# An attention layer's step table: one comparison per unit on VectorE in place of a subtraction on GpSimd and a clamp

## The chip, the cores and the metric

The kernel runs on one core of one Trainium2 chip. The metric is the device time of one launch, in microseconds; the number quoted is the median of three runs. In the profile, PE is TensorE's matmuls and PEld its weight loads, DVE is VectorE, ACT is ScalarE, POOL is GpSimd and SP is the engine that issues most transfers. L423 means line 423 of the kernel's source.

## What is computed

Four graph layers run one after the other over 16 batches of 1024 nodes with 128 features and a sparse adjacency matrix (about 0.8% of the entries, and the diagonal). After each layer comes a residual and a layer norm. The change touches the first layer, an attention over edges:

```python
h_self = x @ W_self + b_self
h_nb = x @ W_nb + b_nb
pre = (h_self @ A1_i)[:, :, None, :] + (h_nb @ A1_j)[:, None, :, :] + A1_b
scores = (relu(pre) @ A2_w)[..., 0] + A2_b[0]
scores = where(adj == 0, -1e9, scores)
attn = softmax(scores, axis=-1)
out = relu(h_self + einsum("bij,bjf->bif", attn, h_nb))
x = layernorm(x + out)
```

## The kernel before

The attention works on edges and not on the full matrix. The 1024 nodes of a batch are cut into 10 groups of 104 rows. A *unit* is a pair of groups (i, j) with j at or after i; 11 units make a *block* (two rows of the triangle of pairs), 5 blocks make a batch, and so there are 80 blocks. For each unit the edges between the two groups are packed into at most 128 slots. For that the kernel counts the edges in each row, turns the counts into running offsets (`off`, one number per row and unit, written by `copy_offsets` from PSUM), and builds from them a *step table* `g`: for each row and each of 128 slots, 1 where the slot lies beyond the row's offset and 0 otherwise. A matmul with a difference matrix (`steps`, L464) turns the step table into a one-hot table: which row owns which slot. A second matmul and a comparison (`others`, `copy_others`, L488) give the other end of each edge; `widen` (L494) makes both tables wider for the gather.

With these tables a unit is worked through as follows: `gather` (L554, L559) fetches the projected features of both ends of 128 edges with matmuls into a PSUM tile `pg`, of which there are three; `score` (L571, DVE) makes the scores; `weigh` (L581, L583, ACT) takes the exponential and multiplies; `scatter` (L592, PE) adds the weighted rows into three PSUM banks, using a table `we` that `numbered` makes (L539, DVE).

Beside this, the next batch is prepared: `mask_rows` (L316, L318, POOL) turns loaded adjacency rows into a 0/1 mask that is kept and stored, `projection` (L343 to L371) makes the features. And the batch before is ended: `collect` (L603), `end_divide`, `end_group` (L636, L639, and the row statistics of L78 and L79), `end_root` (POOL), `end_norm` (ACT), transposes and stores. The ending falls into the first three blocks of the following batch.

The order on every engine is written out by hand. Each piece of work is put into a list with `do(slot, key, f, ...)`; one slot is one unit, and the key is the place in slots from the block's start. The list is sorted by this place (L803), the instructions are emitted in that order, and `as_traced` ties each engine to it. For the block two ahead (`x + 2`) the constants of the change stand here: `BEYOND` (L157) places the subtraction `beyond` (L419, instruction L423 on POOL) and `CLAMP` (L158) the clamp `clamp` (L428, instruction L431 on DVE). Both work in three pieces of 4, 4 and 3 units, that is 512, 512 and 384 columns on 105 partitions. Of `g` there is one buffer, so the first subtraction of a block waits until the last `steps` matmul of the block before has read it. `off` is float32, `k_next` (the numbers 1 to 128 in every partition) and `g` are float16.

```python
BEYOND = (3.72, 5.65, 6.42)
CLAMP = (6.38, 8.56, 11.15)
```

Of the kernel before, what the change touches and what calls it, by code (L numbers as in the profile page):

```python
# [17 lines left out]
ALU = mybir.AluOpType  # L18
# [74 lines left out]
NG, W, C = 10, 104, 128  # L93
NP = NG * W
E = W + 1
# [10 lines left out]
def band(r):  # L106

    return [(i, j) for i in (r, NG - 1 - r) for j in range(i, NG)]
# [45 lines left out]
PROJECT = (  # L154
    (6.25, 6.42, 6.54, 7.25, 7.33, 6.85, 16.48), (9.85, 9.9, 10.6, 9.95, 11.38, 11.56, 17.53),
)
BEYOND = (3.72, 5.65, 6.42)  # L157
CLAMP = (6.38, 8.56, 11.15)  # L158
NUMBERED = (1.38, 5.32, 9.9)
ONE_WAY = (-2.25, 5.95)  # L160
WIDEN = (3.38, 6.02, 8.53)
# [16 lines left out]
def phase_att(ctx, tc, t, c, x1_d, x1T_d, mask_d, keep, flags):  # L178

    nc = tc.nc  # L180
# [10 lines left out]
    def load(name, shape, dtype=F16):  # L191
        w = (cp if name == "k_id" else ep).tile(shape, dtype, name=name)
        nc.sync.dma_start(w, t[name])
        return w
# [12 lines left out]
    k_next = load("k_next", [P, C])  # L207
# [178 lines left out]
    def pieces():  # L386
        return [(n0, min(4, UNITS - n0)) for n0 in range(0, UNITS, 4)]

    def block(x):

        if x not in V and x < B * BANDS:
            v = V[x] = Consts()
            v.x = x
            b, v.r = divmod(x, BANDS)
            v.d, v.mt, v.q, v.todo = S[b], MT[b % 2], QS[x % 2], band(v.r)
        return V.get(x)
# [22 lines left out]
    def beyond(v, n0, m):  # L419

        if n0 == 0:
            v.g = sm.tile([P, UNITS, C], F16, name="g", bufs=1)
        nc.gpsimd.tensor_tensor(  # L423
            v.g[:E, n0 : n0 + m, :], k_next[:E].unsqueeze(1).to_broadcast([E, m, C]),
            v.off[:, n0 : n0 + m].unsqueeze(2).to_broadcast([E, m, C]), ALU.subtract,
        )

    def clamp(v, n0, m):  # L428

        g = v.g[:E, n0 : n0 + m, :]  # L430
        nc.vector.tensor_scalar(g, g, 1.0, 0.0, op0=ALU.min, op1=ALU.max)  # L431

    def ranks(v, n0, m, pw):

# [16 lines left out]
    def one_way(v, half):  # L451

        i = (v.r, NG - 1 - v.r)[half]
        at, nb = half * (NG - v.r), NG - i
        junk = sm.tile([P, NG, W], BF16, name="one_way", bufs=1)
        nc.vector.scalar_tensor_tensor(  # L456
            junk[:W, :nb, :], v.q[:W, at : at + nb, :W], EDGE,
            v.mt[:W, i, i * W : NP].rearrange("p (n w) -> p n w", w=W),
            op0=ALU.is_ge, op1=ALU.not_equal, accum_out=seen_one_way[:W, v.x, half : half + 1],
        )  # L460
# [32 lines left out]
    def widen(v, n0, m):  # L493
        nc.scalar.copy(v.ends[:W, n0 : n0 + m], v.o[:W, n0 : n0 + m])  # L494
# [21 lines left out]
    def bank_products(parts):  # L516

        bank = ps_w.tile([P, 512], F32, name="pw")
        at = 0
        for kind, k, v in parts:  # L520
            f, g = PARTS[kind]
            args = pieces()[k] if kind in ("step", "other", "rank") else ()
            f(v, *args, bank[:, at:])
            held[kind, k, v.x] = lambda g=g, v=v, args=args, to=bank[:, at:]: g(v, *args, to)
            at += TAKES.get(kind, 384)
# [176 lines left out]
    def do(slot, key, f, *args):  # L702
        todo.append((slot + key, len(todo), f, args))
# [39 lines left out]
    for x in range(-3, B * BANDS):  # L743
        b, r = divmod(x, BANDS)
        at = x * UNITS
        for u in range(UNITS if x >= 0 else 0):
            do(at + u, 0.2, open_gather, b, r, u)
            do(at + u, SCORE, take, score, b, r, u)
            do(at + u, WEIGH, take, weigh, b, r, u)
            do(at + u, SCATTER, scatters, b, r * UNITS + u)  # L750
        for k in range(3 if x >= 0 else 0):
            do(at, NUMBERED[k], numbered, b, r, *CHUNKS[k])
        for key, parts in BANKS:
            parts = [(kind, k, x + AHEAD[kind]) for kind, k in parts if 0 <= x + AHEAD[kind] < B * BANDS]
            if parts:
                do(at, key, lambda parts: bank_products([(kind, k, block(y)) for kind, k, y in parts]), parts)
                for kind, k, y in parts:
                    do(at, READ[kind, k], lambda *key: held.pop(key)(), kind, k, y)
        for k in range(3):
            if 0 <= x + 2 < B * BANDS:  # L760
                do(at, BEYOND[k], lambda y, k: beyond(block(y), *pieces()[k]), x + 2, k)
                do(at, CLAMP[k], lambda y, k: clamp(block(y), *pieces()[k]), x + 2, k)
            if 0 <= x + 1 < B * BANDS:
                do(at, WIDEN[k], lambda y, k: widen(block(y), *pieces()[k]), x + 1, k)
        for k in range(2):
            if 0 <= x + 1 < B * BANDS:
                do(at, ONE_WAY[k], lambda y, k: one_way(block(y), k), x + 1, k)
            if 0 <= x and b + 1 < B:
                s = ORDER[2 * r + k]
                do(at, PROJECT[k][0], make, b + 1, s)  # L770
                for i, key in enumerate(PROJECT[k][1:]):
                    do(at, key, step, b + 1, s)
    for b in range(B - 1):
        at = (b + 1) * SLOTS
# [1683 lines left out]
def kernel(ctx: ExitStack, tc: tile.TileContext, t, out):  # L2458
# [29 lines left out]
    for name, shape in (  # L2488
        ("q_less", [P, P]), ("q_slot", [P, P]), ("q_same", [P, P]), ("q_run", [P, N]), ("q_node", [P, T, P]),
        ("q_one_up", [P, P]),  # L2490
    ):
        keep.q[name] = qp.tile(shape, F16, name=name)
    phase_att(tc, t, c, x1_d, x1T_d, mask_d, keep, flags)
    with tc.tile_pool(name="late", bufs=1, side="right") as lp:
        ys = [lp.tile([P, T, F], F32, name=f"y{i}") for i in range(2)]
# [68 lines left out]
```

## Time and profile before

| what | value |
|---|---|
| time, median of three runs | 2974.85 us (2974.74 to 2977.59) |
| the profiled execution, whole | 2983.48 us |
| its span, first to last instruction | 2981.2 us |
| PE busy over the span | 2695.8 us, 90% |
| DVE busy | 2246.4 us, 75% |
| ACT busy | 1845.1 us, 62% |
| POOL busy | 1261.2 us, 42% |
| L423, subtraction on POOL | 240 instructions, 241.9 us |
| L431, clamp on DVE | 240 instructions, 85.2 us |
| L316, mask step on POOL | 150 instructions, 421.7 us |
| L539, `we` on DVE | 240 instructions, 254.4 us |
| L571, score on DVE | 1600 instructions, 398.4 us |

Durations in the profile come from one execution. A busy time is the union of the instructions' durations; instructions of one engine may overlap a little at their ends, so the distance from one start to the next can be shorter than a duration. Shares over the whole span mix four layers; the attention takes about the first 1530 us, and its engines are much fuller than the whole: between 300 and 450 us, for example, PE is busy 143.75 of 150 us, DVE 126.12, ACT 126.59 and POOL 78.81.

### The profile page before, as it was taken

To read this page: it belongs to the slowest core of one execution; us is meant where nothing else is said; L and a number is where in the kernel's file an instruction comes from. 1 tells how busy PE (TensorE), PEld (TensorE's weight loads), DVE (VectorE), ACT (ScalarE), POOL (GpSimd) and SP (SyncE) were. 2 spreads that over 40 slices of the span, in tenths; PEclk is the share of its full clock that TensorE was granted. 3 is DMA by queue.
4 is the path that set the end of the run, shared out by engine and by line. 5 is a ranking of instruction groups with operands and counts; after the bars stand their busy time and mean duration, and the time that the engine had idled before them with its cause. 6 is when DMAs were issued, how large, how long until landed. Compare 5 with 4: busy or idle time off the path is not lost. (4 is left out here: it accounts for less than half of the span.)

```text
span 2981.2 us, 71230 instructions
## 1 busy us (share of the span) xinstructions
PE 2695.8 (90%) x25811; PEld 2407.9 (81%) x25811; DVE 2246.4 (75%) x8654; ACT 1845.1 (62%) x5689; POOL 1261.2 (42%) x1305
## 2 busy tenths in 40 slices
PE   5999999999999999999997888668897999999997
PEld 3888888888888888888897887457786999999996
DVE  5798888988888888988884467756655667777674
ACT  3887888888887888888873233246753433443333
POOL 3655555644555555654223323244433233333321
PEclk8999999999999999999997777789998999999999
DMA  5324332333224332333215442044555254444540
GB/s 160 91 79 114 87 89 68 101 103 84 82 75 115 87 92 73 93 107 88 61 51 168 167 133 79 21 153 170 181 194 212 100 186 177 151 144 181 186 156 17
DMA packets 179962, 348.64 MB, mean 117 GB/s; under 512 B 14148, under 2 KB 89942, under 8 KB 179472
## 3 DMA queue, kind: packets, MB, share of 16 engines
q1 hardware_dynamic: 173584, 328.15, 34.3%
q0 software_dynamic: 4864, 11.63, 1.3%
q10 hardware_dynamic: 1152, 4.19, 0.5%
q8 instruction: 207, 3.39, 0.5%
q14 instruction: 155, 1.27, 0.1%
HBM read 257.87 MB, written 87.03 MB: 116 GB/s over the span
## 5 line engine op out<-in xcount | busy, mean ns | idle before, releaser
L583 ACT ACTIVATE hg<-pg,hg 128x128 f32<-128x128 f32 x1600 | 511.3, 365 | 28.7
L554 PE MATMUL pg<-parts,oh 104*128 104x384 f32 (+1 forms) x1760 | 521.0, 377 | 0.9 <-ACT hg L583 0.8
L316 POOL TENSOR_SCALAR arena<-ld 104x1024 f16<-104x1024 f32 (+1 forms) x150 | 421.7, 2812 | 234.1 <-DMA ld<-in_adjT 234.1
L592 PE MATMUL pa<-hg,we 128*104 128x129 f32 (+1 forms) x3520 | 517.7, 271 | 0.4 <-DVE we L539 0.4
L592 PEld LDWEIGHTS pa<-hg,we 128*104 128x104 f32 x3520 | 465.4, 171 | 10.2 <-DVE we L539 0.8
L571 DVE SCALAR_TENSOR_TENSOR junk<-pg,w_a 128x128 bf16<-128x128 f32 x1600 | 398.4, 283 | 96.9 <-PE pg L559 94.9
L559 PE MATMUL pg<-parts,oh 104*128 104x384 f32 (+1 forms) x1760 | 438.4, 330 | 0.0
L423 POOL TENSOR_TENSOR g<-k_next,off 105x512 f16<-105x512 f16 (+1 forms) x240 | 241.9, 1027 | 315.4 <-PE pw L464 291.7
L559 PEld LDWEIGHTS pg<-parts,oh 104*128 104x128 f32 x1760 | 313.9, 190 | 0.1
L554 PEld LDWEIGHTS pg<-parts,oh 104*128 104x128 f32 x1760 | 276.5, 192 | 27.6 <-issue 15.1
L1667 POOL TENSOR_TENSOR rstd<-ve,mhalf 128x4 f32<-128x4 f32 x96 | 98.1, 1022 | 440.4 <-DVE ve L1666 440.4
L581 ACT ACTIVATE hg<-sc 128x2 f32<-128x2 f32 (+1 forms) x880 | 189.9, 216 | 151.4 <-DVE junk L571 146.7
L1705 ACT COPY xT<-pt 128x512 f32<-128x512 f32 x64 | 37.5, 586 | 374.9 <-PE pt L1704 343.0
L539 DVE TENSOR_TENSOR we<-k_id,ids 128x832 f32<-128x832 f16 (+1 forms) x240 | 254.4, 1060 | 0.0
L494 ACT CAST oh<-oh_b 104x1024 fp32r<-104x1024 bf16 (+1 forms) x240 | 235.2, 980 | 2.4 <-DVE oh_b L488 2.4
L343 PE MATMUL pw<-w_all,xT 128*104 128x512 f32 x320 | 170.2, 613 | 14.2 <-DMA xT<-in_xTp 9.3
L488 DVE TENSOR_TENSOR oh_b<-pw,k_slot_edge 104x512 bf16<-104x512 f32 (+1 forms) x240 | 153.8, 641 | 15.8 <-PE pw L480 15.4
L364 DVE TENSOR_TENSOR parts<-pw,parts 104x384 fp32r<-104x384 f32 x160 | 88.3, 552 | 86.5 <-ACT own L360 85.6
L473 ACT CAST oh_b<-pw 104x512 bf16<-104x512 f32 (+1 forms) x240 | 131.1, 547 | 0.7 <-PE pw L464 0.3
L571 DVE DVE_READ_ACCUMULATOR junk<-pg,w_a 128x1 f32 x1600 | 131.0, 82 | 0.0
L456 DVE SCALAR_TENSOR_TENSOR one_way<-qs,arena 104x1040 bf16<-104x1040 f16 (+9 forms) x160 | 125.7, 786 | 2.2 <-ACT qs L449 2.2
L1508 DVE BATCH_NORM_STATS2 stats<-pt 128x6 f32<-128x512 f32 x120 | 79.0, 691 | 62.6 <-PE pt L1504 61.4
(368 smaller groups left out, 6477.3 us busy)
## 6 DMA issues: line engine op xcount, KB each, us to landing
ld<-in_adjT SPq DMA_DIRECT2D x135, 416.0 KB
keep_adj<-in_adjT SPq DMA_DIRECT2D x8, 4096.0 KB
adj<-in_adjT SPq DMA_DIRECT2D x8, 4096.0 KB
mask_d<-arena SPq DMA_DIRECT2D x144, 208.0 KB
hT_d<-uT SPq DMA_DIRECT2D x48, 512.0 KB
h<-hT_d SPq DMA_DIRECT2D x48, 512.0 KB
arena<-mask_d SPq DMA_DIRECT2D x11, 2048.0 KB
hT<-hT_d SPq DMA_DIRECT2D x32, 512.0 KB
```

Source lines behind the costliest of these rows:

```text
L316: engine.tensor_scalar(mt[:n, s, :N], ld[:n], 0.0, None, op0=ALU.is_gt)
L343: nc.tensor.matmul(pw[:W], d.xT[:, s * W : (s + 1) * W], w_all, start=True, stop=False, skip_group_check=True)
L423: nc.gpsimd.tensor_tensor(v.g[:E, n0 : n0 + m, :], k_next[:E].unsqueeze(1).to_broadcast([E, m, C]), v.off[:, n0 : n0 + m].unsqueeze(2).to_ ...
L488: nc.vector.tensor_tensor(v.o[:W, n0 : n0 + m, 1, :], pw[:W, : m * C].rearrange("p (n c) -> p n c", c=C), k_slot_edge[:W].unsqueeze(1).to_ ...
L494: nc.scalar.copy(v.ends[:W, n0 : n0 + m], v.o[:W, n0 : n0 + m])
L539: nc.vector.tensor_tensor(we[:, :n, :], k_id.unsqueeze(1).to_broadcast([P, n, W]), V[b * BANDS + r].ids[:, 2 * lo : 2 * hi].unsqueeze(2).t ...
L554: nc.tensor.matmul(flat[:, first : 3 * F], own, d.parts[i][:W, p, first:], start=p == 0, stop=False, skip_group_check=True,)
L559: nc.tensor.matmul(pg[:, 1::step, :], other, reversed_parts(d.parts[j][:W, p, :], step), start=False, stop=p == 1, skip_group_check=True,)
L571: nc.vector.scalar_tensor_tensor(junk, pg[:, 1 + e, :], 0.0, w_a2, op0=ALU.max, op1=ALU.mult, accum_out=d.sc[:, at + e : at + e + 1],)
L581: nc.scalar.activation(hg[:, :ways, F], d.sc[:, at : at + ways], AF.Exp)
L583: nc.scalar.activation(hg[:, e, :F], pg[:, 3 - 3 * e, :], AF.Copy, scale=hg[:, e, F : F + 1])
L592: nc.tensor.matmul(PA[bank][:W, at : at + part.stop - part.start], we[:, 2 * (u - lo) + e, :], hg[:, e, part], start=False, stop=True, ski ...
```

## The change

The subtraction on POOL and the clamp on DVE are taken out. In their place DVE compares, once for each unit, the row of slot numbers with that unit's column of offsets: 1 where `k_next` is greater than `off`, else 0. Offsets and slot numbers are whole, so the clamped difference and the comparison are the same table. The three pieces now hold 4, 4 and 3 instructions of 128 columns, and `BEYOND` has the places that `CLAMP` had. The rest of the order stays.

```diff
-BEYOND = (3.72, 5.65, 6.42)
-CLAMP = (6.38, 8.56, 11.15)
+BEYOND = (6.38, 8.56, 11.15)
...
         if n0 == 0:
             v.g = sm.tile([P, UNITS, C], F16, name="g", bufs=1)
-        nc.gpsimd.tensor_tensor(
-            v.g[:E, n0 : n0 + m, :], k_next[:E].unsqueeze(1).to_broadcast([E, m, C]),
-            v.off[:, n0 : n0 + m].unsqueeze(2).to_broadcast([E, m, C]), ALU.subtract,
-        )
-
-    def clamp(v, n0, m):
-
-        g = v.g[:E, n0 : n0 + m, :]
-        nc.vector.tensor_scalar(g, g, 1.0, 0.0, op0=ALU.min, op1=ALU.max)
+        for n in range(n0, n0 + m):
+            nc.vector.tensor_scalar(v.g[:E, n, :], k_next[:E], v.off[:, n : n + 1], None, op0=ALU.is_gt)
...
                 do(at, BEYOND[k], lambda y, k: beyond(block(y), *pieces()[k]), x + 2, k)
-                do(at, CLAMP[k], lambda y, k: clamp(block(y), *pieces()[k]), x + 2, k)
```

## The prediction

> **What bounds the kernel now.** I read the page first: the chain of work that ended last covers only the last 20 us of the final layer, so it says nothing of the attention stage (about 50 to 1530 us), the only place where the change acts. There PE, DVE and ACT are all nearly full, so I cut the stage into its blocks (22 gather weight loads each) and asked for the busy time of each engine in five successive blocks, one batch. Columns: stretch; its length; then busy time (instruction count) of PE, PE weight load, DVE, ACT, POOL; clock; DMA.
>
> ```profile
> core 0: us, PE busy (x) PEld busy (x) DVE busy (x) ACT busy (x) POOL busy (x), PEclk, DMA share, GB/s
> 817.10:836.50 19.40, 18.58 (x161) 15.71 (x160) 18.84 (x88) 15.30 (x52) 12.66 (x12) 1.00 0.58 158
> 836.50:855.00 18.50, 17.92 (x158) 15.23 (x157) 17.68 (x75) 14.73 (x50) 12.70 (x10) 1.00 0.35 96
> 855.00:875.90 20.90, 19.33 (x162) 17.05 (x160) 19.29 (x83) 15.55 (x52) 12.62 (x11) 0.92 0.22 65
> 875.90:893.30 17.40, 17.28 (x157) 15.09 (x156) 12.78 (x60) 17.08 (x57) 6.20 (x5) 1.00 0.00 1
> 893.30:912.50 19.20, 18.43 (x167) 15.92 (x166) 13.04 (x64) 17.01 (x57) 6.23 (x5) 1.00 0.41 116
> ```
>
> In blocks 0, 1 and 2 of a batch (the ones that also end the batch before) DVE idles 0.56, 0.82 and 1.61 us, gaps of its own pipeline included: an order of work fixed on a full engine, so I count time added to DVE there one for one. In block 3 PE (0.12 us idle) and ACT (0.32) are full and DVE idles 4.6; in block 4 DVE idles 6.2. The waits say the same: of the first line's stretch 855 to 876, ACT sits waiting for DVE's score; of the second's, 893 to 912.5, DVE waits for PE.
>
> ```profile
> ACT hg L581 <- DVE junk L571: 3.2, 3, 2.8
> ...
> DVE junk L571 <- PE pg L559: 3.8, 6, 1.4
> ```
>
> **The operations that go.** From the rows of tile g (nanoseconds minimum/median/maximum):
>
> ```profile
> L423 POOL TENSOR_TENSOR g<-k_next,off x240: 820/1038/1285, 48.9 to 1519.9; 105x512 f16<-105x512 f16 x80, 105x384 f16<-105x384 f16 x40
> L431 DVE TENSOR_SCALAR g<-g x240: 245/287/1141, 50.0 to 1532.2; 105x512 f16<-105x512 f16 x80, 105x384 f16<-105x384 f16 x40
> ```
>
> The clamp's median is 287 and its maximum 1141. The timeline shows why: DVE instructions stand while POOL works.
>
> ```profile
> 861.71 1.04 POOL L423 TENSOR_TENSOR g<-k_next,off 105x512 f16<-105x512 f16 x1
> 861.90 2.73 DVE L539 TENSOR_TENSOR we<-k_id,ids 128x832 f32<-128x832 f16 x1
> 862.71 2.77 POOL L316 TENSOR_SCALAR arena<-ld 104x1024 f16<-104x1024 f32 x1
> ...
> 877.15 1.01 DVE L539 TENSOR_TENSOR we<-k_id,ids 128x832 f32<-128x832 f16 x1
> ```
>
> L539 needs 1.01 alone and took 2.73: it stood 1.72 us, through the rest of L423 and 0.87 us of L316.
>
> **What the Trainium skill says.** "SBUF — State Buffer", section "SBUF: two separate sides": VectorE and GpSimd share one port pair under an exclusive lock; a DVE instruction in a two-port mode or with two SBUF inputs blocks fully against a GpSimd instruction and the other way round. The trace agrees for L423; not wholly for L316, which held L539 for 0.87 of its 2.77 us. "VectorE: DVE Perf Modes", section "The perf-mode tier table (the rule you actually need)": a 16-bit tensor_scalar in SBUF runs four elements a cycle, fp32 two. The clamp agrees: 512 elements at four a cycle of 0.96 GHz are 133 ns, leaving 154 fixed. The same page, section "The TRN2 errata — SBUF-src ops pay a fixed extra latency per instruction": many small tiles pay the fixed part each; this is what 11 instructions instead of 3 will do. None of these places prices a per-partition scalar, which the trace does.
>
> **The price of one new instruction.** The trace before has no f16 comparison with a scalar column, but three relatives: L1349 (128 f32, one column), L262 (256, one column), L1671 (128 f32, two columns), and a run of four of the last.
>
> ```profile
> L1349 DVE TENSOR_SCALAR keep_wl<-wl,keep_bn x3: 279/279/280, 2072.3 to 2272.4; 128x128 f32<-128x128 f32 x3
> L262 DVE TENSOR_SCALAR rows<-part,ident x1: 348/348/348, 21.1 to 21.1; 128x256 f32<-128x256 bf16 x1
> L1671 DVE TENSOR_SCALAR x<-x,mv,rstd x256: 312/340/347, 2299.7 to 2944.6; 128x128 f32<-128x128 f32 x128
> 2299.66 1.11 DVE L1671 TENSOR_SCALAR x<-x,mv,rstd 128x128 f32<-128x128 f32 x4 [1.16 <-POOL rstd L1667]
> 2300.69 0.68 DVE L1690 TENSOR_TENSOR x<-x,pp 128x512 f32<-128x512 f32 x1
> ```
>
> 348 - 279 = 69 ns for 128 more elements, two a cycle; so 210 are fixed, 56 more than the clamp's 154. Two columns: 340 - 69 - 154 = 117, again some 58 each. A new instruction (128 f16 at a quarter cycle: 33) lasts 154 + 57 + 33 = 244. Neighbours overlap: four L1671 follow each other in 1.03 us, 257 each, 83 less than their duration. So each takes 161 ns of DVE. Bounds: 0.10 if the column cost nothing in a run, 0.195 if only two elements a cycle were got.
>
> **The sum, part by part, for a batch of five blocks.**
> - Added in blocks 0 to 2: 3 x 11 x 0.161 = 5.31 us of DVE.
> - Removed there, clamps at their undisturbed rate: 3 x (2 x 0.204 + 0.17) = 1.73 (287 - 83, and 0.25 - 0.08 for the piece of three).
> - Removed there, standing behind L423: in block 0 the clamp at 827.71 took 0.91, so 0.62; in block 1 L639 at 843.51 took 1.01 against 0.29, so 0.72; in block 2 L539 above. There L316, freed of L423, would start when L318 ends, at 861.75, and hold to 862.62; L539 would still stand 0.72, so 1.00 goes. Together 2.34.
> - Blocks 0 to 2: 5.31 - 1.73 - 2.34 = +1.24.
> - Block 3: PE and ACT have queues; DVE idles for 2.1 us soon after. 0, or up to 0.44 if the cover is gone.
> - Block 4: three bursts. The first (before 809) runs into 1.5 us of DVE idleness, the third into 0.3. The second is exposed, as the timeline shows: the clamp, L456 and the score stand in a row, and PE's next gather waits for that score.
>
> ```profile
> 813.77 0.29 DVE L431 TENSOR_SCALAR g<-g 105x512 f16<-105x512 f16 x1
> 813.97 1.12 DVE L456 SCALAR_TENSOR_TENSOR one_way<-qs,arena 104x936 bf16<-104x936 f16 x1
> ...
> 815.02 0.28 DVE L571 SCALAR_TENSOR_TENSOR junk<-pg,w_a 128x128 bf16<-128x128 f32 x1
> ...
> 815.69 0.30 PEld L554 LDWEIGHTS pg<-parts,oh 104*128 104x128 f32 x2 [0.30 <-DVE junk L571]
> ```
>
> A burst of four is 4 x 0.161 - 0.204 = 0.44 longer: +0.44.
> - POOL loses 242 us (L423) and its long wait for the buffer g. Its own idleness is worth nothing; it matters only through the lock. The comparison now waits in DVE's queue for off (ACT, made a block earlier) and for the last reader of g (L464, some five slots before), both past by then: 0. Its reader L464 comes at least 1.3 slots later, about 2 us: 0. Queued behind it are the scores that ACT waits for; that is the cost counted above. No DMA is moved.
>
> Total 1.24 + 0.44 = 1.68 us a batch. Fifteen batches have a predecessor to end: 25 us. The first batch and the tail count as nothing. The profiled execution (span 2981.2, whole 2983.5) becomes about 3009; the median of the runs, 8.6 lower, 2975 + 25 = 3000.
>
> **Rivals.**
> - *The cost is hidden* (0.12): PE is busy 18.58 of 19.40, 17.92 of 18.50 and 19.33 of 20.90 us in blocks 0 to 2, so PE could be the true bound and DVE merely close to it; the net 1.24 is less than the 3 us that PE idles. Against it: ACT waits up to 2.8 us for scores there. Time: 2975.
> - *The mask step moves out of the way* (0.24, faster): with L423 and its waits gone, POOL runs L316 as soon as its load has landed, and the locks that L316 puts on DVE fall elsewhere. What stands behind it in this batch: L539 0.72, L456 at 847.12 0.84 (1.31 against 0.47 for 312 elements by its larger shapes), L636 at 829.82 0.43, and 0.34 at the place of 763.57: 2.33 us. If all of it goes, 1.68 - 2.33 = -0.65 a batch: 2965. It decides once more than 1.68 of the 2.33, seven tenths, go. For it: POOL is empty enough to move them. Against: 48 of the 118 mask steps between 300 and 1500 us already wait for their load, not for L423, and moved locks can also land on the new two-port comparisons. The cheap bound of 0.10 an instruction helps this side: alone it gives about -8 us, 2967.
> - *Dearer instructions* (0.16): two elements a cycle, 0.195 each, make blocks 0 to 2 +2.4 and the exposed burst 0.58, and block 3 shows another 0.58: 3.5 a batch, +53, 3028.
>
> **How the numbers follow.** The forecast itself has 0.48, with its own range 2985 to 3015. What can be told from no change here is 0.2%, 6 us. Faster 0.24, same 0.12, slower 0.48 + 0.16 = 0.64. The range takes in the dear end and the faster mechanism but for their outer parts: 2962 to 3030.
>
> **What would show it.** Right: new instructions of about 244 ns, 161 apart; blocks 0 to 2 longer by 0.2 to 0.6 each with DVE idling no more than now; block 4 longer by 0.4; L539 never above 1.9. Wrong: new instructions about 185 or 280 ns; blocks 0 to 2 of unchanged length with PE fuller; or L539, L456 and L636 at their undisturbed 1.01, 0.47 and 0.35 throughout, which would be the mask step's doing.

## The result, and the profile after

The changed kernel takes 2967.67 us (median of five runs, 2962.43 to 2968.89) against 2977.59 for the kernel before (2974.74 to 2982.67): a ratio of 0.9952, 95% interval 0.9939 to 0.9966. It is 10 us faster; 25 us slower were forecast. The time lies in the stated range, on the side of its faster rival.

The profiled execution went from 2983.48 to 2968.89 us. Of these 14.6 us the attention stage has 9.2: from the first gather matmul to the end of the last it took 1500.7 us before and takes 1491.5 now. The rest, 5.4 us, lies outside it, mostly in layers that the change does not touch, and is less than the 8 us by which the five runs of the kernel before differ.

The busy time of each engine in five successive blocks, a batch, of the changed kernel (columns as before: stretch; length; PE, PE weight load, DVE, ACT, POOL; clock; DMA):

```profile
core 0: us, PE busy (x) PEld busy (x) DVE busy (x) ACT busy (x) POOL busy (x), PEclk, DMA share, GB/s
812.00:832.40 20.40, 18.80 (x163) 15.86 (x161) 20.16 (x95) 15.29 (x51) 9.67 (x9) 1.00 0.59 153
832.40:850.10 17.70, 17.64 (x159) 15.18 (x157) 17.29 (x81) 14.78 (x49) 9.79 (x7) 1.00 0.34 93
850.10:869.10 19.00, 18.34 (x161) 15.55 (x160) 18.59 (x89) 15.23 (x50) 8.72 (x6) 1.00 0.28 79
869.10:887.50 18.40, 17.56 (x158) 15.16 (x156) 15.44 (x71) 17.76 (x58) 3.80 (x5) 1.00 0.01 1
887.50:906.80 19.30, 18.53 (x169) 16.03 (x168) 14.35 (x72) 17.11 (x57) 3.33 (x2) 1.00 0.44 120
```

The reader should see three things. Block 1 is now as long as PE needs: 17.64 of 17.70. Block 2 is 1.9 us shorter than the block shown before; that block was a long one of its kind, as is shown below. Block 3 is 1 us longer, and PE, which had idled 0.1 us in it, idles 0.8.

The rows of tile g and of `we` in the changed kernel, and of `we` in the kernel before (nanoseconds minimum/median/maximum):

```profile
L423 DVE TENSOR_SCALAR g<-k_next,off x880: 233/249/1128, 51.1 to 1523.2; 105x128 f16<-105x128 f16 x176
...
L531 DVE TENSOR_TENSOR we<-k_id,ids x240: 797/1009/1850, 63.5 to 1549.4; 128x832 f32<-128x832 f16 x80, 128x624 f32<-128x624 f16 x40
```
```profile
L539 DVE TENSOR_TENSOR we<-k_id,ids x240: 796/1015/2730, 63.7 to 1559.2; 128x832 f32<-128x832 f16 x80, 128x624 f32<-128x624 f16 x40
```

A comparison has a median of 249 ns; 244 were forecast. Undisturbed, they follow each other by 0.163 us in runs (four in 0.65), where 0.161 was forecast. So the price of the new instruction was right. And the `we` of block 2, which took 2.5 to 2.7 us in every one of the fourteen batches of the table below, no longer stands for 1.7 us.

For the rest of this document one table carries the argument. It has the mean length in us of each of the five blocks of a batch, over the second to the fifteenth batch of a trace, measured from a block's first gather matmul to the next block's. The first two rows are the two kernels, the others the experiments below.

| kernel | block 0 | 1 | 2 | 3 | 4 | batch |
|---|---|---|---|---|---|---|
| before | 19.81 | 18.52 | 20.02 | 17.46 | 19.28 | 95.1 |
| changed | 19.93 | 17.79 | 19.05 | 18.32 | 19.28 | 94.4 |
| before, subtraction left out | 19.50 | 17.36 | 18.23 | 17.48 | 19.26 | 91.8 |
| changed, subtraction put back idle | 20.32 | 19.18 | 21.58 | 18.26 | 19.95 | 99.3 |
| changed, compared twice in blocks 0 to 2 | 21.86 | 21.41 | 25.16 | 20.94 | 19.15 | 108.5 |
| changed, compared twice in blocks 3, 4 | 23.34 | 17.76 | 19.13 | 18.32 | 19.72 | 98.3 |
| changed, third piece early | 19.87 | 18.19 | 19.15 | 18.24 | 19.28 | 94.7 |
| compared on POOL throughout | 19.23 | 17.24 | 18.18 | 18.75 | 19.29 | 92.7 |
| POOL in blocks 0, 1 | 19.43 | 17.24 | 18.91 | 18.32 | 19.26 | 93.2 |
| POOL in blocks 0, 1, 2 | 19.48 | 17.24 | 18.16 | 18.68 | 19.25 | 92.8 |
| the same, third piece of block 2 on DVE | 19.39 | 17.24 | 18.16 | 17.52 | 19.25 | 91.6 |
| the same, third piece behind the root | 19.24 | 17.24 | 18.18 | 20.28 | 19.01 | 94.0 |

Before and after differ by 0.7 us a batch: minus 0.73 in block 1 and 0.97 in block 2, plus 0.12 in block 0 and 0.86 in block 3, nothing in block 4.

The mean of block 2 before, 20.02, hides two kinds. In eight of the fourteen batches this block takes 19.37 us on average, in the other six 20.89. Here is one of each (the first is the block that the prediction shows, cut at its gather matmuls), then 3.4 us out of the first:

```profile
855.03:875.86 20.83, 19.26 (x162) 16.98 (x160) 19.22 (x83) 15.48 (x51) 12.62 (x11) 0.92 0.22 65
951.98:971.23 19.25, 17.66 (x161) 15.40 (x160) 18.66 (x80) 15.26 (x51) 11.70 (x9) 1.00 0.24 73
868.30:871.70 3.40, 3.40 (x17) 3.37 (x16) 3.19 (x17) 3.19 (x14) 0.00 (x0) 0.51 0.28 88
```

In both blocks PE waits 1.6 us for the comparison of L488, which stands in DVE's queue behind the long L539. In the first, 1.3 us after this wait has ended, the granted clock falls to half for 3.4 us. PE is then busy 1.6 us longer (19.26 for 17.66) with the same work and idles no longer than in the other; and only in this block does DVE wait for PE in turn. The waits of the first block (who waited for whom; us in total, times, longest):

```profile
PE pw L436 <- DVE oh_b L488: 1.6, 1, 1.6
...
DVE junk L571 <- PE pg L559: 1.1, 2, 0.9
```

It is so in all six. A stretch at half clock costs 1.5 us there, 0.65 us a batch over the fourteen, 9.2 us in the six: as much as the attention stage gained in this pair of traces. In these batches neither of the two traces of the changed kernel has such a stretch, and in its block 2 PE has no wait longer than 0.9 us. Over all traces below they come in the five kernels where PE waits often for 1.2 us or more (11 to 62 times in the fourteen batches), and in none of the others, where it does so once at most. What decides after which of these waits the clock falls stays open (14 waits and 6 stretches before), and no run changes the clock by itself. For executions without a trace only the mean clock is on record: on the chip of the last three runs below, the kernel before takes from 2974 us at a clock of 0.954 to 2989 at 0.950, the changed one 2966 to 2972 at 0.953 to 0.956. At the same 0.954 the changed kernel is still 5 to 8 us the faster, so elsewhere part of the gain may be of another kind.

### The profile page after: what moved, and what is told of

The parts are those of the page before. It is cut to its first block, busy times and chain, and to the rows that moved or that the text cites. A ratio compares the mean times of both kernels' runs of the same rounds, so it can differ in the third digit from the quotient of the medians.

```text
span 2967.0 us, 71688 instructions
## 1 busy us (share of the span) xinstructions
PE 2700.4 (91%) x25811; PEld 2405.0 (81%) x25811; DVE 2299.9 (78%) x9294; ACT 1852.1 (62%) x5689; POOL 1020.9 (34%) x1065
## 5 line engine op out<-in xcount | busy, mean ns | idle before, releaser
L531 DVE TENSOR_TENSOR we<-k_id,ids 128x832 f32<-128x832 f16 (+1 forms) x240 | 229.3, 956 | 0.0
L423 DVE TENSOR_SCALAR g<-k_next,off 105x128 f16<-105x128 f16 x880 | 205.2, 308 | 0.5 <-PE pw L456 0.4
L1723 PE MATMUL pg<-v,adj 128*128 128x128 f32 x1024 | 122.7, 278 | 1.6 <-ACT v L1718 1.3
```

Source lines behind the costliest of these rows:

```text
L423: nc.vector.tensor_scalar(v.g[:E, n, :], k_next[:E], v.off[:, n : n + 1], None, op0=ALU.is_gt)
L531: nc.vector.tensor_tensor(we[:, :n, :], k_id.unsqueeze(1).to_broadcast([P, n, W]), V[b * BANDS + r].ids[:, 2 * lo : 2 * hi].unsqueeze(2).t ...
```

## The experiments

The theory after the result was that the gain is the port pair: without the subtraction, DVE no longer stands behind POOL. The rivals were that PE is the bound and hides the added DVE time (cover), and that POOL helped by no longer waiting for the buffer g before its mask steps (order). Ratios are to the kernel before on the same chip.

**The lock put back, without its result.** The changed kernel, plus POOL's subtraction into a buffer that nobody reads:

```diff
+        nc.gpsimd.tensor_tensor(
+            v.spare[:E, :m, :], k_next[:E, : C - 4].unsqueeze(1).to_broadcast([E, m, C - 4]),
+            v.off[:, n0 : n0 + m].unsqueeze(2).to_broadcast([E, m, C - 4]), ALU.subtract,
+        )
...
+                do(at, (3.72, 5.65, 6.42)[k], lambda y, k: idle_lock(block(y), *pieces()[k]), x + 2, k)
```

> The changed kernel, with the subtraction still issued on POOL at its old places (496 instead of 512 columns), into a spare buffer that nobody reads, so that nothing waits for it. Lock theory (the gain comes from DVE no longer standing behind POOL's subtraction, and behind mask steps that it had delayed): at least the 2.3 to 3.0 us a batch come back, and the new two-port comparisons can stand behind it too; 3005 us, no less than 2990. Cover theory (the added DVE time was hidden by PE, the lock matters little): within 8 us of the changed kernel, 2968. Order theory (what helped is that POOL no longer waits for the buffer g before its mask steps): also about 2968, since this subtraction waits for nothing.

Measured: 3063.2 us, ratio 1.0234 (1.0200 to 1.0269). That is 2.8% above the changed kernel's ratio, some 84 us, for an instruction that nobody waits for. As reasons for the gain, cover and order both fall; a part of cover comes back below, where the added DVE time is paid at half. The timeline of its block 1 shows the cause:

```profile
878.36 2.99 POOL L429 TENSOR_TENSOR spare<-k_next,off 105x496 f16<-105x496 f16 x3
...
879.56 1.06 DVE L640 SCALAR_TENSOR_TENSOR x_rows<-own,x_rows 104x128 f32<-104x128 f32 x1
...
883.66 1.53 DVE L423 TENSOR_SCALAR g<-k_next,off 105x128 f16<-105x128 f16 x4
...
886.12 0.29 DVE L640 SCALAR_TENSOR_TENSOR x_rows<-own,x_rows 104x128 f32<-104x128 f32 x1
```

The same L640 takes 1.06 while POOL subtracts and 0.29 later. The run of four comparisons at 883.66 takes 1.53 instead of 0.65: the new comparisons stand behind POOL as well (there it is a mask step). The cost is larger than expected because the comparisons are victims too: their mean rose from 309 to 369 ns. Five of the fourteen batches also have a stretch at half clock in block 2 (22.80 us on average, 20.90 without). POOL is also busier in this run, which could be a rival to the lock; the comparison on POOL, below, loads POOL more and is faster.

**The removal alone.** The kernel before, without the subtraction; the clamp reads the slot numbers:

```diff
-        nc.gpsimd.tensor_tensor(
-            v.g[:E, n0 : n0 + m, :], k_next[:E].unsqueeze(1).to_broadcast([E, m, C]),
-            v.off[:, n0 : n0 + m].unsqueeze(2).to_broadcast([E, m, C]), ALU.subtract,
-        )
...
-        g = v.g[:E, n0 : n0 + m, :]
-        nc.vector.tensor_scalar(g, g, 1.0, 0.0, op0=ALU.min, op1=ALU.max)
+        g, k = v.g[:E, n0 : n0 + m, :], k_next[:E].unsqueeze(1).to_broadcast([E, m, C])
+        nc.vector.tensor_scalar(g, k, 1.0, 0.0, op0=ALU.min, op1=ALU.max)
```

> The kernel before without POOL's subtraction; the clamp stays, in three pieces, and reads the slot numbers instead of the difference, so the step table is not that of the reference. This is the removal alone. By the terms of the prediction's sum only the waits behind L423 go, 2.34 us a batch: 35 us, ratio 0.988. If each of these waits cost more than its own length (mask steps that come early enough afterwards, PE and DVE no longer waiting for each other), 3.5 to 5.5 us a batch go: ratio 0.972 to 0.982. If the lock is not what the changed kernel gained from: 0.997 or more.

Measured: ratio 0.9801 (0.9786 to 0.9816), 59 us; in the table 3.2 us a batch, 0.31, 1.16 and 1.79 in blocks 0, 1 and 2. This run cuts the change in two: the removal is worth 2.0%, and the comparisons in place of the clamps cost the other way, from 0.9801 to 0.9952, 1.5%, 45 us. In the sum these two had been 35 and 60. Inside the attention stage of the traces the two are smaller, 46 and 37 us; the rest of the ratios lies outside it or in how executions differ. The clock is at full in all these batches, and 0.65 of the 3.2 us are the half-clock stretches that are gone. Without them the removal is worth 2.6 us a batch (1.1 of it in block 2), and the comparisons that replace the clamps cost 2.5.

**DVE time where DVE is full, and where it is not.** Every comparison issued twice, once in blocks 0 to 2 (shown) and once in blocks 3 and 4 (the same with `in (3, 4)`):

```diff
+            if v.x >= 2 and (v.x - 2) % BANDS in (0, 1, 2):
+                nc.vector.tensor_scalar(v.g[:E, n, :], k_next[:E], v.off[:, n : n + 1], None, op0=ALU.is_gt)
```

> The changed kernel with every comparison issued twice in the blocks 0, 1 and 2 of a batch (by the place where it stands in the order), 33 instructions of 0.163 us more a batch, 5.4 us. One-for-one theory (DVE is the bound there): 16 batches x 5.4 = 86 us, 3050 us, and at least 3035. Cover theory (PE is the bound and hides DVE time): under 25 us, below 2993.

> The changed kernel with every comparison issued twice in blocks 3 and 4, 22 instructions more a batch, 3.6 us. The profile of the changed kernel has DVE idle for 3.0 and 4.9 us there. If idle DVE time covers it, only the third piece of block 3, for whose step matmul PE already waits, costs: about 0.5 us a batch, 8 us, 2976. If bursts of comparisons are exposed wherever they stand (scores late, PE's gather late), three bursts of 0.5 to 0.65 us in each block: 3.6 us a batch, 3024.

Measured: 1.0659 (1.0636 to 1.0682) and 1.0131 (1.0107 to 1.0154). Both doses were larger than meant: a second comparison that rewrites what the first has just written follows it by 0.29 us, that is, only after it has ended, and not by 0.163 (eight take 1.81 us).

```profile
943.59 0.25 DVE L423 TENSOR_SCALAR g<-k_next,off 105x128 f16<-105x128 f16 x1
943.88 0.25 DVE L425 TENSOR_SCALAR g<-k_next,off 105x128 f16<-105x128 f16 x1
944.04 0.25 DVE L423 TENSOR_SCALAR g<-k_next,off 105x128 f16<-105x128 f16 x1
```

Counted from the start of each run of comparisons to the next instruction of DVE, the first kernel spends 12.1 us a batch more on the step table than the changed kernel, and takes 14.2 more. But PE now waits long and often, and the clock is at half for 9.5 us a batch. At the 1.5 us that a stretch of 3.4 cost above, this is some 4 us (an estimate from these traces); it leaves about 10 us for 12.1, near to one for one. The second spends 2.3 more in block 3 and 3.1 in block 4, and these blocks grow by 0.00 and 0.44. Its loss is in block 0, into which the doubled third piece of block 4 falls (at 11.15 slots it belongs to the next block): 1.5 us more comparing, 3.4 us longer. Nine of the fourteen batches have half clock in that block; in the five others it is 2.5 us longer. So DVE time is nearly free in blocks 3 and 4 and dear in 0 to 2.

**Block 3's loss.** The timeline of the changed kernel where block 3 begins:

```profile
869.74 1.36 DVE L423 TENSOR_SCALAR g<-k_next,off 105x128 f16<-105x128 f16 x3
...
869.82 2.82 POOL L315 TENSOR_SCALAR arena<-ld 104x1024 f16<-104x1024 f32 x1
...
871.15 0.10 PEld L456 LDWEIGHTS <-k_step 105*128 105x128 f16 x1 [0.72 <-DVE g L423]
871.25 0.32 PE L456 MATMUL pw<-g,k_step 105*128 105x384 f16 x1 [0.50 <-ACT oh_b L465]
```

Three comparisons take 1.36 us instead of 0.49, since a mask step starts between them, and the step matmul waits for them. The third piece was moved ahead:

```diff
-BEYOND = (6.38, 8.56, 11.15)
+BEYOND = (6.38, 8.56, 10.3)
```

> The changed kernel with the third piece of the comparisons at 10.3 slots instead of 11.15. In the changed kernel's profile the third piece of block 2's work runs at the start of block 3, stands 0.7 us behind a mask step, and PE waits 0.7 us for it; block 3 is 0.86 us a batch longer than before. If that new wait is what block 3 lost, the move gives back 0.5 to 0.9 us a batch there, and in block 0 the 0.5 us that the third piece of block 4 takes, against 0.5 us more in block 2: about 10 us, ratio to the kernel before 0.991 to 0.993. If block 3 is longer because DVE comes late out of block 2, nothing is gained: 0.995.

Measured: 0.9962 (0.9948 to 0.9976), not faster; block 3 18.24. PE's waits in its block 3 (who waited for whom; us in total, times, longest):

```profile
PE pw L456 <- ACT hg L575: 0.5, 1, 0.5
PE pw L472 <- ACT qs L441: 0.4, 1, 0.4
PEld L456 <- PE pg L551: 0.7, 1, 0.7
```

The wait for g is gone and the block is as long: PE now waits for ACT. The new wait was seen rightly and was not what set the block's length.

**The comparison on POOL.** One instruction a unit on POOL, at the subtraction's places:

```diff
-            nc.vector.tensor_scalar(v.g[:E, n, :], k_next[:E], v.off[:, n : n + 1], None, op0=ALU.is_gt)
+            nc.gpsimd.tensor_scalar(v.g[:E, n, :], k_next[:E], v.off[:, n : n + 1], None, op0=ALU.is_gt)
```

> The comparison made by POOL and not by DVE, one instruction a unit, at the old places of the subtraction. DVE is freed of some 11 us a batch. If POOL's comparison with a scalar column takes about 0.4 us each and holds the port pair little, as a one-input POOL instruction may, blocks 0 to 2 come down to what PE needs (17.7 to 18.4 each) and block 3 to 17.4: some 2 to 3 us a batch, 2930 us. If it holds the lock as the subtraction did: near the kernel before, 2975. If POOL takes over 1 us each, the table is late for the step matmul and the time rises above 3000.

Measured: 0.9915 (0.9893 to 0.9936). POOL needs 600 ns for each, 6.6 us a block, and yet DVE is freed: `we` never takes more than 1.72 us in that trace, where it had taken 2.73. Blocks 0 to 2 come down to 19.2, 17.2 and 18.2, lower than without any subtraction, but block 3 rises to 18.75. In these three blocks POOL idles 2.5, 2.3 and 0.7 us, against 7.9, 5.3 and 11.1 in the run with the lock put back, where a batch takes 6.6 us more: it is not POOL's load that costs there, but what its two-input subtraction does to DVE. From here on the question was which block should compare where:

```diff
+        engine = nc.gpsimd if (v.x - 2) % BANDS in (0, 1) else nc.vector
         for n in range(n0, n0 + m):
-            nc.vector.tensor_scalar(v.g[:E, n, :], k_next[:E], v.off[:, n : n + 1], None, op0=ALU.is_gt)
+            engine.tensor_scalar(v.g[:E, n, :], k_next[:E], v.off[:, n : n + 1], None, op0=ALU.is_gt)
...
+                keys = (3.72, 5.65, 6.42) if x % BANDS in (0, 1) else (6.38, 8.56, 10.3 if x % BANDS == 4 else 11.15)
```

> Comparisons on POOL in blocks 0 and 1, where DVE is full, and on DVE in blocks 2, 3 and 4, with the third piece of block 4 at 10.3 slots so that it stays out of block 0. Against the comparison on POOL alone (0.9915): block 3 loses its 1.3 us (POOL no longer hands over the table late), block 2 has 1.3 us of comparisons on a full DVE. If both theories hold (DVE counts one for one in blocks 0 to 2, is free in 3 and 4; POOL's comparison hardly holds the port): blocks 17.4 to 19.3, together 92.5 us, ratio 0.987. If POOL's comparisons were good only because POOL did all of them: 0.992 to 0.995.

> The same with POOL in blocks 0, 1 and 2. Block 2 keeps POOL's 18.2 us; block 3 starts with the table of block 2 still late from POOL (idle for only 0.7 us in block 2), so it keeps part of its 1.3 us unless POOL, freed in blocks 3 and 4, is early by then. Together 91.8 to 92.6 us a batch, ratio 0.982 to 0.989; if block 3's loss comes from block 2's backlog alone, no better than 0.990.

Measured: 0.9900 (0.9885 to 0.9915) both times: short of the first's 0.987 and just above the second's 0.982 to 0.989. With DVE comparing in block 2, block 2 is 18.91 and block 3 is 18.32, as in the changed kernel; with POOL comparing there, 18.16 and 18.68. In the second case another wait is at work in block 3:

```profile
PE pw L473 <- ACT oh_b L466: 1.1, 1, 1.1
...
ACT x_rows L650 <- POOL shift L644: 1.1, 1, 1.1
```

POOL is at the third piece when the root of the layer norm becomes due; ACT waits for the shift that follows from it, PE for ACT. Two ways out of it, the third piece of block 2 on DVE, or on POOL behind the root:

```diff
-        engine = nc.gpsimd if (v.x - 2) % BANDS in (0, 1, 2) else nc.vector
+        engine = nc.gpsimd if (v.x - 2) % BANDS < (3 if n0 < 8 else 2) else nc.vector
...
+                keys = ((3.72, 5.65, 6.42), (3.72, 5.65, 6.42), (3.72, 5.65, 10.3), (6.38, 8.56, 11.15), (6.38, 8.56, 10.3))[x % BANDS]
```

> Comparisons on POOL in blocks 0, 1 and 2, but the third piece of block 2 on DVE at 10.3 slots; blocks 3 and 4 on DVE. In the run with POOL in blocks 0 to 2, POOL works at that piece when the layer norm's root of the batch before becomes due, and in block 3 ACT waits 1.1 us for POOL's shift and PE 1.1 us for ACT. If that is what block 3 loses, it falls from 18.7 to 17.5 to 17.9 us, block 2 takes at most 0.5 more: together 91.8 to 92.3 us a batch, ratio 0.983 to 0.987. If not, 0.990 again.

> The same, but the third piece of block 2 stays on POOL, at 8.6 slots, behind the root. ACT's wait for the shift goes; the third piece ends some 2.5 us later, about when its step matmul is due in block 3. Ratio 0.983 to 0.987 if it is in time, 0.990 if PE now waits for it.

> The changed kernel once more, on the chip of the two runs above, to compare them with it there: 0.995 to the kernel before.

Measured on one chip: 0.9820 (0.9802 to 0.9838) with the third piece on DVE, 0.9952 (0.9935 to 0.9968) with it on POOL behind the root, 0.9955 (0.9939 to 0.9971) for the changed kernel. The first is 2929.32 us, 40 below the changed kernel and 54 below the kernel before, the shortest time of the kernels that leave nothing out. Two blocks of it, 2 and 3:

```profile
833.10:851.30 18.20, 17.81 (x161) 15.54 (x159) 17.67 (x78) 14.90 (x49) 16.74 (x16) 1.00 0.40 113
851.30:869.10 17.80, 17.48 (x158) 15.17 (x156) 14.65 (x68) 17.43 (x58) 4.25 (x5) 1.00 0.01 2
```

Block 3 still has two pieces of comparisons on DVE and idles PE for only 0.3 us. So it is not comparing in block 3 that lengthens it; what comes late out of block 2 is left as the reason. The second way fails by its own wait:

```profile
PE pw L457 <- POOL g L424: 2.0, 1, 2.0
```

In eight of the fourteen batches half clock comes on top: block 3 takes 21.18 us with such a stretch, 19.09 without.

## Why the prediction was wrong, step by step

The sum had +1.68 us a batch; measured are -0.71. Of the 2.4 us between them 1.5 are what the comparisons cost in place of the clamps, 0.65 the clock, which had no term, and 0.25 the waits behind the subtraction.

- *Price of a comparison* (0.161 us a piece in a run): right, 0.163.
- *DVE is full in blocks 0 to 2 and has room in 3 and 4*: right in the main. Doubling shows it: 14.2 us for 12.1 in the first (some 4 of them the clock), 0.44 for 5.4 in the second.
- *What the comparisons cost in blocks 0 to 2* (5.31 - 1.73 = 3.58 us a batch, counted one for one): this step failed most. From the run without the subtraction to the changed kernel these blocks grow by 0.43, 0.43 and 0.82, together 1.68, though the table takes 3.25 us a batch more of DVE there. Once the waits are gone DVE is no longer the bound in every block: without the subtraction block 1 had PE idle for 0.02 us. These first 3.25 us of DVE are therefore paid at half the rate, the next 12 at nearly the full one. Comparisons also stand behind POOL, by 1.3 us in these three blocks together (6.7 us from start to next instruction, where 33 of 0.163 would take 5.4); the clamps, in the run without the subtraction, lose no less.
- *What goes with the subtraction* (the term of 2.34 us a batch, 35 us): too small, 3.2 measured. The waits themselves were nearly right: without the half-clock stretches the removal gives 0.31, 1.16 and 1.14 us in blocks 0, 1 and 2, where the sum had 0.62, 0.72 and 1.00, together 2.6 for 2.34. The comparison of the two traces, instruction group by group, shows for block 2 L539 1.4 us shorter a batch, not 1.00; for block 1 L639 0.62, L456 0.28 and L539 0.17. So mask steps did move off some of these instructions, as the faster rival had it. What the sum put at nothing is the clock: 0.65 us a batch of half-clock stretches in block 2, which go with PE's wait behind the long L539. The prediction's own line for that block shows it, with a clock of 0.92; the block was one of the six and not of the eight.
- *Block 3 at nothing*: wrong, 0.84 us a batch. About half of what blocks 0 to 2 did not pay is paid here. That the visible wait for g is not the reason is shown by the early third piece (wait gone, 18.24), and that comparing in block 3 is not, by POOL doing two pieces of block 2 with the third early (17.52). DVE coming late out of block 2, with ACT and PE both full in block 3 and unable to catch up, fits all of these runs; none delays DVE alone.
- *Block 4's exposed burst, 0.44*: wrong, 0.00. PE's 0.3 us before the gather that was named as its price stand in all of these kernels, twice as many comparisons included; it was not DVE's time that they showed. What sets block 4's length stays open.

The errors point one way. Removal 3.2 instead of 2.3, comparisons 2.5 (1.68 and 0.84) instead of 3.6 and 0.44: together -0.7 where the sum had +1.7. The faster rival gave -0.65 and 2965 us, close to what was measured, but by luck: it kept the full price of the comparisons and had no clock, and of its mask steps moving off only some tenths of a microsecond a batch are seen (L456, and L539 beyond 1.00).

## What to carry to other kernels

When a full engine stands behind another one's port lock, take the lock away in an experiment of its own before pricing what replaces it: here the removal was worth 59 us, the replacement cost 45, and the sum read from one batch had the sign of the difference wrong. Read the same block in several batches, the clock column with it: the block from which the largest wait was read had 3.4 us at half clock, and eight of fourteen like it had none. Price added work on a nearly full engine one for one only as far as no other engine becomes the bound, and look for the unpaid part in the next stretch. Then split the work by stretch: engines are free in different blocks, and the best of these kernels gives each block's comparisons to the engine that is free there.

## What was not expected of the hardware

- A one-input comparison on POOL with a scalar column took 600 ns for 128 f16 elements, about 60% of what the two-input subtraction took for 512, and blocked DVE far less for it: with 6.6 us of it in every block, blocks 0 to 2 were 0.05 to 0.27 us shorter than with no subtraction and the clamps on DVE. The Trainium skill, "SBUF — State Buffer", section "SBUF: two separate sides", has GpSimd instructions hold the pair for their whole length; the two-input subtraction did (DVE's `x_rows` step, 0.29 us undisturbed, took 0.80 to 1.02 beside it in the kernel before), the one-input comparisons here did not (0.29 to 0.40 in the 63 cases where one runs beside it), nor did most mask steps (a median of 0.29 beside 75 of them, with 1.01 at most).
- Two comparisons on DVE, the second writing what the first wrote, follow each other by 0.29 us, against 0.163 for comparisons that write side by side.
- In the kernel before, six of PE's fourteen waits of 1.2 to 1.7 us in block 2 were followed, 0.7 to 1.8 us after their end, by 3.4 us at half the granted clock. A wait that had come from another engine's port lock thus cost about as much again, 1.5 us, when it was already over.
